# A decoder layer whose attention shares TensorE with projections: eight single-bank PSUM tiles in two sets that change places

## The chip, the cores and the metric

The kernel runs on one core of a Trainium2 chip. The core has a matrix engine (TensorE, called PE in the profile), a vector engine (DVE), an engine for activation functions (ACT), a general engine (POOL) and an engine that only issues transfers (SP). Matrix products are written into PSUM, a memory of eight banks of 2 KB for each of 128 partitions, so that one bank holds a tile of 128x512 in fp32. The metric is the time of one execution in device microseconds. Before the change it was 678.75 us (median of three, 678.59 to 678.98).

## The reference, cut to what matters

The kernel computes one pre-norm decoder layer for two sequences of 512 tokens and a width of 1024, in fp32:

```python
x = x + attention(layernorm(x))        # 32 query heads and 8 key heads of width 32, rope, causal
x = x + cross(layernorm(x), ctx)       # fake_quant(x) @ fake_quant(ctx), ctx is 1024x1024 per sequence
x = x + ffn(layernorm(x))              # x @ W_org.T + a mixture of 8 low-rank experts of rank 64

def attention(x):
    q, k, v = split(x @ w_qkv.T + b_qkv)                   # 1024, 256 and 256 columns
    scores = rope(q) @ rope(k).T / sqrt(32)                # each key head serves four query heads
    attn = softmax(where(causal, scores, -1e20))
    return (attn @ v) @ w_o.T + b_o
```

The change touches the attention and what runs beside it. The cross product and the feed-forward part fill the tail of the program; some of their units can also be used as filling work.

## The kernel before

**An order written by a planner.** The program does not leave the order to a scheduler. While it is built, a small model of the engines (class `Clocks`, line 99) keeps an estimated time for each engine, and the program text decides from it which instruction comes next. On the chip PE, DVE, ACT and POOL each execute their own list strictly in that order and wait on semaphores for one another. Work that is not TensorE's, such as rope, sums of weights and quantisation, lies in `lanes` of `Hop`s; `dispatch` (line 449) takes a hop when its engine is free and its operands are ready by the model, and `force` takes one at once. Work that is TensorE's and belongs to no slot lies in `queue` as generators; `step` (481) takes one matmul from the first generator that may start, `fill(us)` (527) adds to a `credit` and steps until it is spent, and `hold(us)` (535) steps until the model's PE clock has reached a time, so that PE doesn't stand still until then. When the queue has nothing, `hold` in the last slots draws from `last_resort`, a generator called `beside` with units of the second sequence's output product and other tail work.

**Chunks and slots.** The 32 heads of a sequence are handled as 8 chunks of 4 heads; with two sequences there are 16 chunks `g`. Four heads of width 32 use the 128 rows of TensorE together: four matmuls, each on 32 rows. Two chunks form a pair, and a pair takes five slots (`NS`), so that there are 40 slots (`n_slots`). The tables `QUERIES` and `KEYS` say which query tiles and key blocks a slot has; because of the causal mask a query tile `t` has `(t+1)*128` keys, and the slots are composed so that each covers 512 columns in all.

**One slot.** `scores(i)` (999) makes four score tiles `sc` (line 1016, queries by keys). DVE then adds the mask and takes each row's extreme, one instruction per head and part (`ms`, line 1029), and ACT exponentiates and sums (line 1039). When a chunk's slots are done, `split(g)` (1048) takes logarithms of the sums and splits them into three bf16 terms, in a chain over ACT, DVE and POOL; `turn_terms` (1069) transposes these by a DMA on ACT's queue to `mT`. Four slots later (`LAG`), `weights(i-4)` (1085) makes the transposed scores `st` (line 1098, keys by queries) and adds the terms by a matmul of `ones` with `mT` (line 1106), so that one exponential (line 1115, `pt`) gives normalised weights in the orientation that the next product needs. POOL clears the masked corner of the diagonal blocks (line 1118). `attend(g)` (1133) multiplies the weights with the values (`pv`, line 1141) and copies the result to `oT`.

**PSUM.** Three single banks (`ps_mm`) rotate among the filling work's products. One tile of four banks (`ps_sc`) is used by `sc` and `st` in turn; so `st` has to wait until DVE has read all of `sc`, and the next `sc` until ACT has read `st`. One bank (`ps_pv`) is for `pv`. Ahead of the loop and behind it, five further single banks stand in place of the last two pools. The function `mm` (370) hands out a bank for filling work, and `settle` forces its reader into the order if too many banks are unread.

**Filling work.** Queries, keys and values are projected by a Strassen–Winograd scheme, in units of four matmuls of 128x512 (`pj`, line 657, `quarter`), each added by DVE or copied by ACT. After them come the first sequence's output products (`wo`, in `g_tokens` line 1248, and `W_first` line 1726, which adds one chunk's contribution as soon as that chunk's values are there), and its quantised cross product (`cs`, `ct`). A unit may be half done when the slot's own matmuls interrupt it: in the loop, each slot runs `scores`, possibly `attend`, then `fill(rate * SLOT_S[j])`, then `weights`, then `fill(rate * SLOT_T[j])`.

Of the kernel before, what the change touches and what calls it, by code (L numbers as in the profile page):

```python
# [47 lines left out]
SLOT_S = (2.7, 3.2, 0.8, 2.7, 0.8)  # L48
SLOT_T = (1.8, 2.2, 2.2, 1.8, 2.2)
FILL_1 = 116.0  # L50
FILL_2 = 80.0
# [47 lines left out]
class Clocks:  # L99
# [6 lines left out]
    def __init__(self, nc):  # L106
        self.nc = nc
        self.seen = 0
        self.at = {"PE": 0.0, "DVE": 0.0, "Activation": 0.0, "Pool": 0.0, "DMA": 0.0}
        self.written = {}  # L110
        self.read = {}
        self.before = {}
        self.slots = {}
        self.used = {}
        self.tile_size = None

# [26 lines left out]
    def add(self, ins):  # L143
# [69 lines left out]
        for name, part in sources:  # L213
            self.read[name].add(part, done or end, engine)
        self.log(ins, engine, names, start)
# [6 lines left out]
def kernel(  # L222
# [58 lines left out]
    ps_mm = pool("ps_mm", 3, space=PSUM)  # L281
# [7 lines left out]
    beginning = ExitStack()  # L289
    ps_first = pool("ps_first", 5, beginning, space=PSUM)  # L290
# [66 lines left out]
    mm_pools = [ps_mm, ps_first, ps_first, ps_mm, ps_first, ps_first, ps_mm, ps_first]  # L357
    mm_count = [0]

    unread = []  # L360
    opened = [0]

    def settle(n):

        unread[:] = [key for key in unread if key not in done]
        while len(unread) > n:
            force(unread[0])
            unread[:] = [key for key in unread if key not in done]

    def mm(shape, name, dtype=F32):  # L370

        settle(2 if mm_pools[1] is ps_mm else 5)
        mm_count[0] += 1
        return mm_pools[mm_count[0] % len(mm_pools)].tile(shape, dtype, tag="mm", name=name)
# [24 lines left out]
    def transpose_f32(dst, t, src, name):  # L399

        for g in range(NK // 4):
# [5 lines left out]
            evacuate(dst[g][:, :, t * P : (t + 1) * P], ps)  # L407

# [68 lines left out]
    last_resort = [iter(())]  # L477
    weighted = [0]
    attended = [0]

# [19 lines left out]
    def may_start(key):  # L500
        if key == "post":
            return attended[0] >= NC - 1
# [24 lines left out]
    def fill(us):  # L527

        credit[0] += us
        while credit[0] > 0 and any_may():  # L530
            if not step():
                credit[0] = min(credit[0], 3.0)
                break

    def hold(us):

        while clocks.now("PE") + HOLD < us:
            if not (any_may() and step()) and next(last_resort[0], None) is None:
                break
# [99 lines left out]
    def add(col, dst, ps, other, key, bias=None, in_mm=True):  # L639
# [10 lines left out]
        if in_mm:  # L650
            unread.append(key)
# [14 lines left out]
    def g_kept(c, part=WHOLE, bank=None):  # L666
# [5 lines left out]
        if bank is None:  # L672
            unread.append(key)
# [3 lines left out]
        )  # L677

    def g_first(c, part=WHOLE, bank=None):
# [6 lines left out]
        add(c, dst[:, part], ps[:, part], place(c, 1, 0)[:, part], key, 0, bank is None)  # L686
        if last:
            complete(c, 0, 0, dst, key)

    def g_second(c):  # L690
# [7 lines left out]
        add(c, both, ps, both, ("U2", c))  # L698
        if c == COLUMNS[-1]:
# [5 lines left out]
        add(c, more, ps, both, ("U4", c))  # L705
        force(("S", 4))
# [4 lines left out]
        complete(c, 0, 1, dst, ("C12", c))  # L711

    def g_third(cols):

        for c in cols:
# [5 lines left out]
            add(c, more, ps, more, ("U7", c), 1)  # L721
            force(("T", c, 4))
# [3 lines left out]
            complete(c, 1, 0, both, ("C21", c))  # L726
        for c in cols:
# [9 lines left out]
    def g_values(b, halves_):  # L737
# [10 lines left out]
        for half, ps in zip(halves_, banks):  # L748
            evacuate(vs[b][:, :, half * P : (half + 1) * P], ps)
            if not b:  # L750
                q_live[0] -= 1

# [129 lines left out]
    banks = [mm([P, S], f"first_kv{i}") for i in range(4)]  # L882
# [16 lines left out]
    first_kv(slice(2 * P, S))  # L899

# [37 lines left out]
    settle(0)  # L938
    beginning.close()
    mm_pools[:] = [ps_mm] * 3  # L940
    ps_sc = pool("ps_sc", 1, attn, space=PSUM)
    ps_pv = pool("ps_pv", 1, attn, space=PSUM)
# [46 lines left out]
    last_sc = [None]  # L989

    def sc_free():

        clocks.catch_up()
        return clocks.read[last_sc[0].name].last() if last_sc[0] is not None else 0.0

# [3 lines left out]
    def scores(i):  # L999


        pair, j = divmod(i, NS)
        sc = ps_sc.tile([P, 4, S], F32, tag="sc", name=f"sc{i}")
        parts = []
        at_col = 0
# [1130 lines left out]
```

## Time and profile before

| | |
|---|---|
| time, median of three | 678.75 us (678.59 to 678.98) |
| the profiled execution: span from first to last instruction | 675.4 us |
| what lies around that span, against the median | 3.35 us |
| granted TensorE clock, mean | 0.996 |
| first scores of the loop start | 45.8 us |
| last scores of the loop start | 376.6 us |
| last values (`pv`) end | 409.7 us |
| busy PE / DVE / ACT / POOL | 647.2 / 504.2 / 299.3 / 93.5 us |

The profile has one execution of the program, taken by the hardware profiler. The profiled execution's own time is its span of 675.4 us; the small rest up to the median lies ahead of the first and behind the last instruction. An operation's line gives its source line, the engine, and output and inputs by the program's names, with shapes as partitions x elements; behind the bar stand its total busy time, the mean duration of one in ns, and the idle time of its engine just before it with what ended that. In the timeline the first column is the start, the second the time until the group's end, `x8` the number of instructions that stand side by side, and a bracket the idle time before them. An fp32 matmul appears as two records because it takes two passes.

The whole has three parts. The lead-in to 45.8 us normalises the input and makes the first projections. The attention loop runs to 409.7 us. The tail does what is left: the second sequence's output product, most of the cross product and the feed-forward part.

### The profile page before, as it was taken

What the parts mean: (1) busy time and instruction counts of PE and PEld (TensorE: products, weight loads), DVE (VectorE), ACT (ScalarE), POOL (GpSimd) and SP (SyncE); (2) the same over time, 40 slices, a digit from 0 to 9 for tenths busy, and PEclk for the clock granted to TensorE, in tenths of its full rate; (3) what the DMA queues carried; (4) which work ended last, traced back from release to release, by engine and by line L of the source; (5) the groups of instructions that cost most, each with busy time, mean ns of one, the idle gap of its engine ahead of it and who ended that gap; (6) DMA issues with size and microseconds to landing.
All of it is one profiled execution on the core that took longest, in us unless ns stands there. A gap on an engine that the chain in (4) does not pass through costs nothing.

```text
span 675.4 us, 8962 instructions
## 1 busy us (share of the span) xinstructions
PE 647.2 (96%) x3197; PEld 294.5 (44%) x3204; DVE 504.2 (75%) x1205; ACT 299.3 (44%) x695; POOL 93.5 (14%) x213
## 2 busy tenths in 40 slices
PE   5999689999999999999989999999999999999997
PEld 5754233343433434334434444444445454444443
DVE  5799689976678989777678657898969944743775
ACT  2245465666776486877767731354221100110100
POOL 2100023312222122122222321000001000000000
PEclk9999899999999999999999999999999999999999
DMA  9930000010103352102100208295100003000104
GB/s 288 324 74 0 8 9 1 9 40 9 39 2 102 101 134 40 65 14 50 24 10 1 24 9 287 93 333 97 20 28 0 1 31 124 1 0 0 63 0 186
DMA packets 42476, 44.63 MB, mean 66 GB/s; under 512 B 19264, under 2 KB 32576, under 8 KB 42432
## 3 DMA queue, kind: packets, MB, share of 16 engines
q1 hardware_dynamic: 24992, 38.82, 17.3%
q10 hardware_dynamic: 17440, 5.25, 4.8%
q8 instruction: 25, 0.41, 0.3%
q14 instruction: 19, 0.16, 0.1%
HBM read 35.66 MB, written 4.19 MB: 59 GB/s over the span
## 4 chain that ended last, share of the span: by engine, by line
PE 70%; ACT 15%; DVE 12%; issue 1%; DMA 0%; POOL 0%; ACTq 0%; DVEq 0%; POOLq 0%
PE wb L1599 14%; ACT ms L1039 8%; PE pj L657 8%; PE wo L1599 7%; PE up L1682 7%; PE h L1646 7%; ACT pt L1115 7%; DVE ms L1029 5%; PE sc L1016 5%; PE st L1098 3%; PE ct L1248 3%; PE wo L1248 3%; PE first_kv L657 2%; PE pj_v L657 2%; PE pv L1141 2%; PE pj_k L657 1%
## 5 line engine op out<-in xcount | busy, mean ns | idle before, releaser
L1039 ACT ACTIVATE ms<-ms,stats 128x512 f32<-128x512 f32 (+3 forms) x256 | 140.2, 549 | 84.0 <-DVE stats L1029 81.5
L1029 DVE CUSTOM_DVE_ANT_0 ms<-sc,mask 128x512 f32<-128x512 f32 (+3 forms) x256 | 108.3, 485 | 34.8 <-PE sc L1016 31.8
L1115 ACT ACTIVATE pt<-st 128x2048 f32<-128x2048 f32 x40 | 74.8, 1870 | 38.3 <-PE st L1106 38.1
L657 PE MATMUL pj<-xT,wq 128*128 128x512 f32 x192 | 90.9, 606 | 0.0
L1118 POOL TENSOR_SCALAR_AFFINE_SELECT pt<-pt 128x512 f32<-128x512 f32 x64 | 47.4, 757 | 245.2 <-ACT pt L1115 245.2
L1098 PE MATMUL st<-qT,kT 32*128 32x128 f32 (+3 forms) x512 | 49.5, 461 | 4.9 <-DVE stats L1029 4.8
L657 PEld LDWEIGHTS pj<-xT,wq 128*128 128x128 f32 x192 | 33.8, 189 | 40.3 <-issue 39.7
L1016 PE MATMUL sc<-kT,qT 32*128 32x128 f32 (+3 forms) x512 | 45.8, 460 | 4.1 <-ACT pt L1115 1.4
L1039 ACT ACTIVATION_READ_ACCUMULATOR ms<-ms,stats 128x1 f32 x256 | 47.8, 187 | 0.0
L1248 PE MATMUL wo<-wo,oT 128*128 128x512 f32 x96 | 46.6, 613 | 0.0
L1016 PEld LDWEIGHTS sc<-kT,qT 32*128 32x128 f32 x512 | 22.4, 184 | 39.6 <-ACT pt L1115 26.5
L1141 PE MATMUL pv<-pt,v 128*32 128x128 f32 (+3 forms) x512 | 37.8, 436 | 0.0
L1098 PEld LDWEIGHTS st<-qT,kT 32*128 32x128 f32 x512 | 21.1, 185 | 32.6 <-DVE stats L1029 18.8
L1248 PE MATMUL ct<-q,q1T 128*128 128x512 bf16 x123 | 28.0, 379 | 1.3 <-DVE oT L382 0.8
L1599 PE MATMUL wb<-tb,S 128*128 128x512 f32 x64 | 28.3, 595 | 0.0
L1599 PE MATMUL wb<-worg,S 128*128 128x512 f32 x64 | 28.0, 592 | 0.0
L1599 PE MATMUL wb<-worg,x3T 128*128 128x512 f32 x64 | 27.8, 592 | 0.0
L1141 PEld LDWEIGHTS pv<-pt,v 128*32 128x32 f32 x512 | 14.9, 109 | 29.3 <-issue 20.6
L1248 PEld LDWEIGHTS wo<-wo,oT 128*128 128x128 f32 x96 | 16.7, 189 | 21.0 <-issue 20.3
L657 PE MATMUL pj_k<-xT,wk 128*128 128x512 f32 x32 | 17.2, 667 | 5.6 <-DVE qT L648 5.6
L648 DVE TENSOR_TENSOR qT<-pj,qT 128x512 f32<-128x512 f32 x28 | 18.8, 683 | 4.2 <-PE pj L657 4.2
L1189 ACT ACTIVATE raw<-raw,qp_sb,inv_s 128x1024 f32<-128x1024 f32 x8 | 9.8, 1237 | 25.3 <-DMA raw<-in_ctx_dram 24.0
(235 smaller groups left out, 1017.6 us busy)
## 6 DMA issues: line engine op xcount, KB each, us to landing
wq<-in_wqT_dram SPq DMA_DIRECT2D x8, 512.0 KB, 8.7
ctx_raw<-in_ctx_dram SPq DMA_DIRECT2D x8, 512.0 KB, 3.3
wo<-in_woT_dram SPq DMA_DIRECT2D x8, 512.0 KB, 3.3
raw<-in_ctx_dram SPq DMA_DIRECT2D x8, 512.0 KB, 5.7
worg<-in_worgT_dram SPq DMA_DIRECT2D x8, 512.0 KB, 7.1
out_dram<-x SPq DMA_DIRECT2D x16, 256.0 KB, 2.1
x<-in_x_dram SPq DMA_DIRECT2D x7, 512.0 KB, 6.0
x_raw<-in_x_dram SPq DMA_DIRECT2D x4, 512.0 KB, 7.5
```

The costliest lines, as they stand in the source:

```text
L657: nc.tensor.matmul(ps[:, part], weight[:, k, :], xs_[:, k, part], start=(k == 0), stop=(k == n - 1),)
L1016: nc.tensor.matmul(sc[:, s, part], qTs[b, c][row(s), t * P : (t + 1) * P], kTs[b][row(s), c // 4, :klen], start=True, stop=True,)
L1029: nc.vector.tensor_tensor_reduce(out=ms, in0=sc[:, s, part], in1=mask[:, S - klen :], scale=-scale, scalar=BIG, op0=ALU.add, op1=ALU.min, ...
L1039: nc.scalar.activation(ms, ms, AF.Exp, bias=least, scale=-1.0, accum_out=stats[g][:, t, s, 1:2],)
L1098: nc.tensor.matmul(sc[:, s, part], kTs[b][row(s), c // 4, kb * P : (kb + 1) * P], qTs[b, c][row(s), kb * P :], start=True, stop=False,)
L1115: nc.scalar.activation(pt, sc[:, :, :n], AF.Exp, scale=scale)
L1118: nc.gpsimd.affine_select(out=diagonal, in_=diagonal, compare_op=ALU.is_ge, fill=0.0, base=0, pattern=[[0, 4], [1, P]], channel_multiplier=-1,
L1141: nc.tensor.matmul(pv[row(s), kb * P :], vs[b][:, kb, h * HD : (h + 1) * HD], pt[:, s, part], start=(kb == 0), stop=(kb == NT - 1),)
L1248: nc.tensor.matmul(ps, l[:, t * P : (t + 1) * P], r[:, cols], start=(k == 0), stop=(k == len(terms_) - 1))
L1599: nc.tensor.matmul(ps[i], l[:, k, i * P : (i + 1) * P], r(k), start=(k == 0), stop=(k == n - 1))
L1646: nc.tensor.matmul(ps[i], r(k)[:, i * P : (i + 1) * P], l[:, k, :], start=(k == 0), stop=(k == n - 1))
L1682: nc.tensor.matmul(ps[t], l[:, k, t * P : (t + 1) * P], r(k), start=(k == 0), stop=(k == n - 1))
```

## The change

The three PSUM pools become one pool of eight single-bank tiles, `sets[0][0..3]` and `sets[1][0..3]`. Each slot becomes one `visit(i)`. In a visit, `scores(i)` goes into the set called `new`, one head per bank, and `weights(i-4)`, the transposed scores, directly behind it into the set called `old`, which is where the filling units ran since the last visit. Then, head by head, come DVE's minimum and ACT's exponential of the new scores, and ACT's exponential of the transposed scores, now four of 128x512 in place of one of 128x2048. If a chunk's values are due, `pv` goes into the first bank of `new` after DVE's minimum of head 0 has been written into the order. From then to the next visit, filling units may use only the banks of `new`, and only whole units run there: generators yield `CLOSED` at their end, and `close()` steps until no bank is half written. The next visit swaps the sets.

The bookkeeping is changed with it. `take_bank` marks a bank as open, `read_by` names the lane's hop that will read it, and `empty` forces those readers before a set is used. `fill` is given a cycle time less the visit's own share, and rounds to whole units; `hold` adds a unit only if the model's PE clock is more than `HOLD` and half a unit early. The other changes: `post`, the work behind the first sequence's attention, may start only when all eight chunks are attended (before: seven); `W_first` is gone, and every output product of the first sequence is made in two halves of four matmuls with a DVE add each; `last_resort` is gone from `hold`; the loop ends with visits 40 to 43, which hold only transposed scores and values.

Its core as a diff:

```diff
-SLOT_S = (2.7, 3.2, 0.8, 2.7, 0.8)
-SLOT_T = (1.8, 2.2, 2.2, 1.8, 2.2)
-FILL_1 = 116.0
-FILL_2 = 80.0
+VISIT, VALUES = 2.35, 2.35
+CYCLE_1, CYCLE_2 = 7.5, 7.1
+UNIT = 3.44
...
-    ps_mm = pool("ps_mm", 3, space=PSUM)
+    psum = pool("psum", 1, space=PSUM)
...
+    sets = [
+        [psum.tile([P, 512], F32, tag=f"bank{n}{i}", name=f"bank{n}{i}") for i in range(4)]
+        for n in range(2)
+    ]
...
+    def is_free(place):
+
+        n, i = place
+        key = reader.get(place)
+        if key is None or key in done:
+            return True
+        return key is OPEN and clocks.bank_read[sets[n][i].name] >= taken[place]
+
+    def empty(places):
+
+        for place in places:
+            if not is_free(place):
+                assert reader[place] is not OPEN, place
+                force(reader[place])
...
     def may_start(key):
         if key == "post":
-            return attended[0] >= NC - 1
+            return attended[0] >= NC
...
     def fill(us):
 
         credit[0] += us
-        while credit[0] > 0 and any_may():
+        while any_may() and (is_open() or credit[0] > UNIT / 2):
             if not step():
-                credit[0] = min(credit[0], 3.0)
+                credit[0] = min(credit[0], UNIT)
                 break
 
+    def close():
+
+        while is_open():
+            step()
+
     def hold(us):
 
-        while clocks.now("PE") + HOLD < us:
-            if not (any_may() and step()) and next(last_resort[0], None) is None:
-                break
+        while clocks.now("PE") + HOLD + UNIT / 2 < us and any_may() and step():
+            close()
...
-        pt = ptp.tile([P, 4, n], F32, tag=f"pt{j % 3}", name=f"pt{i}")
-        nc.scalar.activation(pt, sc[:, :, :n], AF.Exp, scale=scale)
+
+    def terms_of(i, sc):
+
+        parts = turned(i)
+        n = parts[-1][2].stop
+        pt = ptp.tile([P, 4, n], F32, tag=f"pt{i % NS % 3}", name=f"pt{i}")
+        for s in range(4):
+            nc.scalar.activation(pt[:, s, :], sc[s][:, :n], AF.Exp, scale=scale)
+            yield
...
+        many = len(terms_) if how == "ctx" else len(terms_) // 2
+        for first in range(0, len(terms_), many):
+            part = terms_[first : first + many]
+            ps = mm([P, 512], f"{name}{b}_{t}_{h}")
...
-        hold(when([pts[g, n][0] for n in range(NT)]))
-        attend(g)
-
-    for i in range(n_slots + LAG - 1):
+
+    filler = [0]
+
+    def visit(i):
+
         pair, j = divmod(i, NS)
-        if i == n_slots:
-            last_resort[0] = beside
...
+        old, new = filler[0], 1 - filler[0]
+        g = 2 * pair + j // 2 - 3 if j in (2, 4) else -1
...
+        close()
+        when_free = [last_read((new, s)) for s in range(4)]
         if i >= LAG:
-            of = {2 * ((i - LAG) // NS) + n for n, _ in KEYS[(i - LAG) % NS]}
-            for g in sorted(of):
-                force(("mT", g))
-            hold(max([sc_free()] + [when([mT[g]]) for g in of]))
-            weights(i - LAG)
+            of = {n for n, _, _ in turned(i - LAG)}
+            for n in sorted(of):
+                force(("mT", n))
+            when_free += [when([mT[n]]) for n in of]
+        hold(max(when_free))
+        empty([(old, s) for s in range(4)])
+        of = {}
+        sc, st = sets[new], sets[old]
+        if i < n_slots:
+            scores(i, sc)
+        if i >= LAG:
+            weights(i - LAG, st)
+        exponentials = terms_of(i - LAG, st) if i >= LAG else iter([None] * 4)
+        for s in range(4):
+            if s == 1 and g >= 0:
+                pv = take_bank((new, 0))
+                attend(g, pv)
+            if i < n_slots:
+                least_of(i, sc, s, of)
+                total_of(i, s, of)
+            next(exponentials)
+        for _ in exponentials:
+            pass
+        if g >= 0:
+            attended_to(g, pv)
+        filler[0] = new
+        allowed[:] = [(new, s) for s in range(4)]
         dispatch()
-        fill(rate * SLOT_T[j])
-        hold(sc_free())
+        fill((CYCLE_1 if i <= n_slots // 2 + LAG else CYCLE_2) - VISIT - VALUES * (g >= 0))
...
-    weights(n_slots - 1)
+
+    for i in range(n_slots + LAG):
+        visit(i)
+    close()
+    empty(every)
...
     run_some(4)
-    attend(last - 1)
+    pv = mm([P, S], "pv")
+    attend(last - 1, pv)
+    attended_to(last - 1, pv)
     run_some(5)
```

The order of the instructions in the two programs differs accordingly: in the changed one, 36 times `st` follows `sc` with nothing between, and all units stand whole. The number of passes through TensorE is the same.

## The prediction

> **What bounds the kernel now.** First the page's busy row, its clock row and its chain of work that ended last:
>
> ```profile
> PE 647.2 (96%) x3197; PEld 294.5 (44%) x3204; DVE 504.2 (75%) x1205; ACT 299.3 (44%) x695; POOL 93.5 (14%) x213
> ...
> PEclk9999899999999999999999999999999999999999
> ...
> PE 70%; ACT 15%; DVE 12%; issue 1%; DMA 0%; POOL 0%; ACTq 0%; DVEq 0%; POOLq 0%
> ```
>
> TensorE is the bound at nearly full clock, but 27% of the chain passes through ACT and DVE. The windows' table cuts the span at the first scores (45.8) and at the end of the last values (409.7):
>
> ```profile
> 0.00:45.80 45.80, 38.52 (x196) 28.45 (x196) 34.41 (x80) 12.76 (x25) 7.42 (x21) 1.00 0.86 253
> 45.80:409.70 363.90, 347.81 (x2305) 146.84 (x2308) 277.65 (x819) 240.17 (x608) 80.83 (x183) 1.00 0.14 33
> 409.70:675.40 265.70, 260.89 (x701) 119.19 (x700) 192.16 (x307) 46.38 (x62) 5.30 (x9) 1.00 0.24 79
> ```
>
> The middle stage holds all that is changed. Its busy PE is not all streaming; TensorE's timeline shows what a block of matmuls takes:
>
> ```profile
> 118.43 0.93 PE L1098 MATMUL st<-qT,kT 32*128 32x384 f32 x8 [1.02 <-DVE stats L1029]
> 119.18 0.34 PE L1106 MATMUL st<-mT,onesb 3*128 3x384 bf16 x4
> 119.35 0.40 PE L1098 MATMUL st<-qT,kT 32*128 32x128 f32 x8
> 119.57 0.24 PE L1106 MATMUL st<-mT,onesb 3*128 3x128 bf16 x4
> ...
> 121.84 1.15 PE L1016 MATMUL sc<-kT,qT 32*128 32x384 f32 x16
> 122.92 1.12 PE L657 MATMUL pj<-xT,wq 128*128 128x512 f32 x2
> 123.97 2.36 PE L1141 MATMUL pv<-pt,v 128*32 128x512 f32 x32
> 126.26 1.13 PE L657 MATMUL pj<-xT,wq 128*128 128x512 f32 x2
> 127.32 1.14 PE L1098 MATMUL st<-qT,kT 32*128 32x512 f32 x8
> ```
>
> Weight loads inside a long run of projections come every 0.43 us (0.19 busy, 0.24 idle), so one fp32 pass is 0.43 and a unit of four matmuls (eight passes) 3.43. Two passes between scores and values need 0.86 but take 1.05 (122.92 to 123.97): a change of the kind of matmul costs about 0.21. The key blocks of one `st` are neighbours, and show no such cost. Without it a slot's `sc` needs 0.85, `st` with its ones 1.07, one `pv` 2.13.
>
> The stage needs 184.8 of filling work (projections, output weights, quantised matmuls and transposes, their passes counted in the order of instructions) + 40×0.85 + 40×1.07 + 16×2.13 = 295.7. I count 176 changes of kind, 176×0.21 = 37. So 363.9−295.7−37 = 31 us are waits. By engine the waits are:
>
> ```profile
> ACT pt L1115 <- PE st L1106: 38.1, 20, 7.1
> ...
> DVE ms L1029 <- PE sc L1016: 31.8, 21, 4.3
> ...
> PEld sc L1016 <- ACT pt L1115: 26.5, 29, 1.2
> ```
>
> ACT and DVE wait for PE more than PE for them; `sc` waits for the exponential that frees the one four-bank tile, at most 1.2 us, because half-finished units stand between. One long wait is bad for another reason:
>
> ```profile
> 78.56 4.40 PE L657 MATMUL pj_k<-xT,wk 128*128 128x512 f32 x6 [3.68 <-DVE qT L648]
> ```
>
> Six records take 4.40 there (0.73 each) where 0.43 is usual: the granted clock is half until about 83.1, which is the 8 in the clock row. That costs about 1.7 us on top of the wait. [...]
>
> **The change, part by part.**
>
> *Fewer changes of kind.* In after's order `st` follows `sc` directly (36 times, kinds alike, taken at 0 as between key blocks; at 0.21 it would be +7.6), and units are whole. 95 costing changes remain: 95×0.21 = 20, a gain of 17 us.
>
> *Work moved.* 9.4 us of filling work (two of the quantised blocks and transposes) falls behind the loop: the stage needs 286.3, the tail 256.9+9.4 = 266.3. Neutral in itself. The tail's own 8.8 of waits and changes are kept. The tail receives part of the eight more DVE adds (each half of a W tile now has its own, 0.60 each, +4.8 on DVE in all); DVE is busy 192 of 266 us there and PE 261, so PE covers them; uncovered, +4.8. The lead-in loses banks (four, then eight, against eight): taken at 0, bounds −1 and +3 (its idle PE is 45.8−38.5 = 7.3, mostly on x and its norms). SP has the same transfers; the 16 transposes on ACT's queue (2.4 us to landing) stand behind up to eight exponentials, priced below.
>
> *The split exponential.*
>
> ```profile
> L1115 ACT ACTIVATE pt<-st 128x2048 f32<-128x2048 f32 x40 | 74.8, 1870 | 38.3 <-PE st L1106 38.1
> L1118 POOL TENSOR_SCALAR_AFFINE_SELECT pt<-pt 128x512 f32<-128x512 f32 x64 | 47.4, 757 | 245.2 <-ACT pt L1115 245.2
> ```
>
> One of 128x2048 holds ACT 1.77 start to next start; four of 128x512 have no row. Lower bound: a quarter each, 0.45. Upper: ACT's copy of 128x512 out of PSUM, 0.58. Taken 0.49 (that copy's start-to-start is 0.48): 1.96 a visit, +0.19 a visit, at most +0.55. It counts only where ACT ends a visit. [...]
>
> *The new wait.* Before, a unit could be half done while `st` waited; after, between visits only whole units run, into the banks that `sc` has just left, and the next `sc` needs the banks of the previous `st`, freed by its exponentials, which now alternate with the score exponentials on ACT. Score exponentials run every 0.71 a head at 512 columns (0.61, and 0.09 for the accumulator read) and 0.98 where a head has two parts (235.25 to 236.23 in ACT's timeline: 0.39 and 0.60). ACT's block per visit is 4×(0.71+0.49) = 4.8 or 4×(0.98+0.49) = 5.9. The first exponential starts 1.8 to 2.06 after its `sc`, so the next `sc` cannot finish its last head before about 6.5 or 7.7. PE's own work is 0.85+1.07+0.22 = 2.15 a visit, 4.5 with `pv`, plus 3.43 a unit and 0.2: with two units 9.2 (covered), with `pv` and one unit 8.2 (covered), with one unit 5.8 (short by 0.7 to 1.9), with none 2.1 or 4.5 (short by 2 to 5). After's order gives the units: 16 visits have two, 15 have one or a little more (3.4 to 4.7 us), nine have half a unit or less. Carried from visit to visit with these numbers:
> - exponentials: visits 12, 13, 17, 23, 24 and 35 to 38 follow thin ones and wait 1.7, 2.7, 1.9, 1.9, 4.4, 1.3, 2.2, 1.2, 0.6: 18 us. Visits 22 and 23 are thin because the first half's output weights now wait for the eighth chunk's values, where before they followed each chunk's.
> - `st` waits for DVE's add of the last unit (0.6 to 0.7, queued behind rope and ctx rows of 0.6 to 0.8): mostly 0.3 to 0.9, once 2.6: 10 us. What is queued on DVE behind that add are the minima of the next visit.
> - visits 0 to 3: a unit waits for the minima to read a bank, behind DVE's weight and x sums: 9 us.
> - `mT` landing: 2.
>
> In the loop 39; last scores at 45.8+333 (328 to 339 as I vary the exponential, the DVE load and the 0.21), against 376.6 before.
>
> *The end.* Before, 33 us from the last `sc` to the end of the last `pv`, 16.6 of filling work in it. After has only 3.4 (one output unit): the exponentials of visit 39 end at 7.7, the terms 3.1 later (384.23 to 387.29 before), the transpose lands at 13.3; then `st` 1.2, exponentials 2.0, two selects 1.5 (0.757 each), `pv` 2.4, `st` 1.3, exponentials 2.1, selects 1.5, `pv` 2.3: 27.5. PE needs 15.2 of that: 12 us of waits. Two stops (visit 24, the wait for `mT`) exceed 3.5 us and should halve the clock as at 78.56: 2×1.7 = 3.4.
>
> **The sum**, with W for the stage's waits: 45.8 + 286.3 + 20 + W + 266.3 + 8.8 = 627.2 + W. Before's own 31 would give 658.2; W = 39+12+3.4 = 54 gives 681.6, against 675.4. The profiled execution lies 3.35 under the median of 678.75, so about **685 us**. Break-even is W = 48.
>
> **Rivals.**
> 1. *Waits stay under 46: faster, 662 to 677.* For: the waits' table, where ACT idles 38 us for PE and PE little for ACT; and the 39 is a hand recurrence in which a late head delays everything behind it. If the 9 us of visits 0 to 3 fall by 6 and the 18 halve, W = 39: a span of 666, a time of 669.5. Against: visits with no unit have nothing else to run, whatever the order. It decides at W = 48.
> 2. *ACT's chain sets the loop: 692 to 703.* Exponentials at 0.58 add 0.36 in the dozen or so visits that ACT ends (+4.3), the DVE adds lose their cover (+4.8), the clock drops at four more stops (+6.8): 685+16 = 701. Against: DVE and ACT have long idle times in before.
> 3. *The change does little: 677.4 to 680.1.* Fewer changes of kind and the emptied end cancel: W = 47 to 49.
>
> **How the numbers follow.** 0.2% (1.4 us) is about what a measurement of this kernel can tell from no change. Forecast (680.1 to 692) 0.48; rival 1 0.31; rival 2 0.15; rival 3 0.06. The likeliest is 685, its own range 680 to 692. For 8 in 10 the range runs from 668 (rival 1 without its lowest fifth) to 699 (rival 2 with its three extras not all together). Faster 0.31, same 0.06, slower 0.63.
>
> **What would show it.** Right: PE idle in the stage beyond 20 us, most of it before `sc`, released by ACT's split exponential at visits 12, 13, 17, 23, 24 and 35 to 38, and a gap of some 4 us at visit 24; four exponentials of 0.55 to 0.6 duration a visit; `sc` and `st` back to back without the 0.2; last `sc` near 379, last `pv` near 406; tail near 275; an 8 or lower in the clock row near 250 and 390. Wrong: last `sc` before 370 (waits over-counted), `sc` to `st` costing 0.2 (+7.6), a tail over 280 (DVE adds uncovered), or the clock staying full through the end.

## The result, and the profile after

The changed kernel takes 711.65 us (median of four runs, 710.9 to 714.23) against 678.67 us before: 1.0493 times as long, with an interval of 1.0463 to 1.0522. The direction of the forecast (slower, 685 us) was right. The size was not: the loss is 33 us where 6 were forecast, and the time lies outside the range of 668 to 699.

The page of the changed kernel, its busy row, its clock row and its chain (the same rows as those shown of before):

```profile
PE 677.2 (95%) x3198; PEld 318.9 (45%) x3204; DVE 507.7 (71%) x1210; ACT 307.5 (43%) x818; POOL 89.2 (13%) x213
...
PEclk9999999997999996999999879999999999999999
...
PE 78%; DVE 10%; ACT 8%; issue 2%; DMA 1%; POOL 0%; ACTq 0%; SPq 0%; DVEq 0%; POOLq 0%
```

ACT's share of the chain has halved, from 15% to 8%, and TensorE's has grown from 70% to 78%. Read alone, that looks like a gain, but the time is longer. The clock row says one reason: a 7, a 6, an 8 and a 7 stand where before had one 8. In those slices the granted clock was 0.71, 0.69, 0.83 and 0.75 on the mean, and 0.50 for part of the time, so some of its larger share is work at half speed.

The windows' table of the changed kernel, cut at the first scores and at the end of the last values:

```profile
0.00:45.78 45.78, 37.97 (x197) 28.02 (x197) 34.50 (x80) 12.08 (x24) 7.44 (x21) 1.00 0.84 253
45.78:435.80 390.02, 368.82 (x2258) 166.02 (x2260) 275.98 (x815) 245.81 (x726) 75.88 (x182) 0.95 0.11 31
435.80:710.20 274.40, 270.42 (x749) 124.82 (x748) 197.24 (x316) 49.57 (x68) 5.87 (x10) 1.00 0.23 77
```

The lead-in is unchanged. The tail is 8.7 us longer, which is the work that moved there (9.4 forecast). The attention stage is 26.1 us longer, although it holds 9.2 us less work. The granted clock of the stage, third column from the end, is 0.95.

The place where the first 7 of the clock row comes from, in TensorE's timeline of the changed kernel (visits 12 to 14; start, length, operation, idle before):

```profile
151.13 1.32 PE L1071 MATMUL bank<-kT,qT 32*128 32x256 f32 x6
153.22 0.91 PE L1071 MATMUL bank<-kT,qT 32*128 32x256 f32 x9 [0.77 <-ACT pt L1172]
...
155.35 2.36 PE L1198 MATMUL bank<-pt,v 128*32 128x512 f32 x32
157.64 2.07 PE L1071 MATMUL bank<-kT,qT 32*128 32x512 f32 x4
160.06 1.12 PE L1071 MATMUL bank<-kT,qT 32*128 32x512 f32 x2 [0.34 <-ACT pt L1172]
161.52 1.22 PE L1071 MATMUL bank<-kT,qT 32*128 32x512 f32 x1 [0.34 <-ACT pt L1172]
...
165.66 6.52 PE L707 MATMUL bank<-oT,t 128*128 128x512 f32 x8
172.01 3.60 PE L707 MATMUL bank<-xT,wq 128*128 128x512 f32 x8
```

Visit 12 has no unit of filling work between its values (155.35) and the next scores (157.64). Those scores then come one head at a time: each waits until ACT has freed its bank. Four heads that need 0.85 us together take from 157.64 to beyond 162. Nothing here is an idle stretch of 3 us; TensorE runs one head on 32 of its 128 rows, waits 0.34, runs the next. Yet the granted clock falls at 161.1 and returns at 171.4, and the unit at 165.66 takes 6.52 us where the next takes 3.60. The windows' table, cut at these times (third column from the end: the granted clock):

```profile
157.71:161.12 3.41, 3.07 (x7) 0.81 (x6) 0.69 (x1) 3.41 (x13) 0.00 (x0) 1.00 0.00 0
161.12:171.36 10.24, 9.90 (x34) 5.11 (x34) 5.70 (x15) 6.77 (x16) 3.56 (x10) 0.50 0.06 13
171.36:175.00 3.64, 3.64 (x9) 1.52 (x8) 1.29 (x2) 0.00 (x0) 0.00 (x0) 1.00 0.41 144
```

In the first of these windows ACT is busy for all 3.41 us, and TensorE waits for it. But ACT's own timeline shows that ACT waits in its turn just before and behind: for the scores (through DVE's minimum) and for the transposed scores, which wait for ACT:

```profile
154.55 0.51 ACT L1098 ACTIVATE ms<-ms,stats 128x256 f32<-128x256 f32 x1 [1.38 <-DVE stats L1083]
...
163.04 0.72 ACT L1098 ACTIVATE ms<-ms,stats 128x512 f32<-128x512 f32 x1 [1.22 <-DVE stats L1083]
...
165.72 0.60 ACT L1172 ACTIVATE pt<-bank 128x512 f32<-128x512 f32 x1 [1.87 <-PE bank L1158]
```

It is a ring: last exponential of the old visit, last head of the new scores, transposed scores behind it on TensorE, first exponential of these, and so on. With a unit or two in between, the ring has slack. Without one, every link is on the path.

The waits of the changed kernel that matter here (engine, line, releaser: us in total, times, longest):

```profile
ACT ms L1098 <- DVE stats L1083: 119.0, 40, 6.5
...
DVE ratio L1118 <- ACT ratio L1116: 47.1, 15, 3.5
...
PEld bank L1071 <- ACT pt L1172: 18.5, 23, 1.2
...
DVE ms L1083 <- PE bank L1071: 17.0, 16, 5.4
...
ACT pt L1172 <- PE bank L1198: 15.6, 15, 3.0
...
PEld bank L1150 <- DVE qT L699: 5.9, 8, 1.2
...
PE bank L1158 <- DMA mT<-terms: 4.5, 1, 4.5
```

The wait of the scores' loads for `pt` was 26.5 us in 29 waits before; it has not grown in sum. What has changed is where it stands, in a few visits in a row with nothing else to run. DVE's wait for `ratio` is 47.1 us in 15 waits; it comes back below. In the waits' table of before it was:

```profile
DVE ratio L1059 <- ACT ratio L1057: 14.2, 7, 3.5
```

A sum over the stage, each visit's length less the streaming time of its matmuls at full clock (0.43 us for an fp32 pass of 512 columns, as between the weight loads of before), gives:

| us | before | after |
|---|---|---|
| stage | 363.9 | 390.0 |
| streaming at full clock | 305.1 | 295.9 |
| changes of the kind of matmul | 176 x 0.21 = 37 | 95 x 0.21 + 36 x 0.11 = 24 |
| streaming done at half clock (its extra time) | 1.7 | 14.8 |
| the rest: waits | 20 | 55 |

The price of 0.21 for a change of kind is the forecast's. Visits 5, 11, 16 and 25 of the changed kernel, which hardly wait, leave 0.18 for one; at that price the waits would be 25 before and 58 after.

For the changed kernel the excess over streaming is 94.1 in all; 45.0 of it stands in five places: visits 13 (9.2), 23 (4.3), 24 (8.6), 37 (7.5), and from visit 39 to the last values (15.5). Four of the five follow a visit with half a unit or less; ahead of visit 37 two visits have half a unit each and one has 3.2 us. The other 35 visits have 1.4 each. Those with hardly a wait have 0.5 to 0.6, for the changes of kind; many others wait 0.9 more in `st`. One of these, TensorE's timeline of the changed kernel:

```profile
209.70 1.36 PE L1071 MATMUL bank<-kT,qT 32*128 32x512 f32 x8
210.66 1.42 PE L1150 MATMUL bank<-qT,kT 32*128 32x384 f32 x5
211.50 0.33 PE L1158 MATMUL bank<-mT,onesb 3*128 3x384 bf16 x1
...
212.78 7.13 PE L707 MATMUL bank<-xT,wq 128*128 128x512 f32 x16
```

`sc` starts 0.96 before `st`, that is 0.11 over its 0.85: here the step from `sc` to `st`, both on 32 rows, costs 0.11, less than the 0.21 of a change of kind, but not nothing. `st` then takes from 210.66 to 212.78, 2.12 where 1.2 is usual, because one of its banks still holds the last unit's result. DVE's timeline of the changed kernel says why that is added so late:

```profile
210.28 0.34 DVE L1118 TENSOR_TENSOR ratio<-ratio,stats 128x16 f32<-128x16 f32 x1 [3.38 <-ACT ratio L1116]
...
210.74 0.68 DVE L699 TENSOR_TENSOR qT<-bank,qT 128x512 f32<-128x512 f32 x1
```

The unit is done at 209.7, but on DVE its add stands behind a step of the chunk's `split`, which waits 3.38 us for ACT, and ACT takes that step only after the visit's eight exponentials. So the order of DVE passes ACT's delay on to TensorE, once for each chunk.

### The profile page after: what moved, and what is told of

It reads as the page before. It is cut to its first block, busy times and chain, and to the rows that moved or that the text cites. A ratio compares the mean times of both kernels' runs of the same rounds, so it can differ in the third digit from the quotient of the medians.

```text
span 710.2 us, 9224 instructions
## 1 busy us (share of the span) xinstructions
PE 677.2 (95%) x3198; PEld 318.9 (45%) x3204; DVE 507.7 (71%) x1210; ACT 307.5 (43%) x818; POOL 89.2 (13%) x213
## 4 chain that ended last, share of the span: by engine, by line
PE 78%; DVE 10%; ACT 8%; issue 2%; DMA 1%; POOL 0%; ACTq 0%; SPq 0%; DVEq 0%; POOLq 0%
PE bank L1665 20%; PE bank L707 15%; PE bank L1314 10%; PE bank L1748 7%; PE bank L1712 7%; PE bank L1150 6%; PE bank L1071 5%; PE bank L1198 5%; ACT ms L1098 4%; ACT pt L1172 3%; DVE ms L1083 2%; PE bank L450 2%; PE bank L1158 2%; DVE sh_q L629 1%; DVE qT L699 1%
## 5 line engine op out<-in xcount | busy, mean ns | idle before, releaser
L1083 DVE CUSTOM_DVE_ANT_0 ms<-bank,mask 128x512 f32<-128x512 f32 (+3 forms) x256 | 108.2, 486 | 17.2 <-PE bank L1071 17.0
L1172 ACT ACTIVATE pt<-bank 128x512 f32<-128x512 f32 x160 | 92.7, 588 | 23.6 <-PE bank L1198 15.6
L707 PE MATMUL bank<-xT,wq 128*128 128x512 f32 x192 | 87.6, 599 | 3.2 <-DVE stats L1083 3.2
L1150 PE MATMUL bank<-qT,kT 32*128 32x384 f32 (+3 forms) x512 | 73.1, 474 | 6.1 <-DVE oT L427 1.7
L1071 PE MATMUL bank<-kT,qT 32*128 32x128 f32 (+3 forms) x512 | 68.5, 474 | 5.8 <-ACT pt L1172 5.8
L1314 PE MATMUL bank<-wo,oT 128*128 128x512 f32 x128 | 57.9, 603 | 0.0
L707 PEld LDWEIGHTS bank<-xT,wq 128*128 128x128 f32 x192 | 34.9, 190 | 42.7 <-issue 36.5
L1071 PEld LDWEIGHTS bank<-kT,qT 32*128 32x128 f32 x512 | 31.4, 188 | 48.9 <-ACT pt L1172 18.5
L1150 PEld LDWEIGHTS bank<-qT,kT 32*128 32x128 f32 x512 | 35.5, 195 | 26.0 <-DVE qT L699 5.9
L1198 PE MATMUL bank<-pt,v 128*32 128x128 f32 (+3 forms) x512 | 43.8, 489 | 0.0
L1158 PE MATMUL bank<-mT,onesb 3*128 3x512 bf16 (+3 forms) x256 | 34.6, 315 | 4.5 <-DMA mT<-terms 4.5
L1118 DVE TENSOR_TENSOR ratio<-ratio,stats 128x16 f32<-128x16 f32 x16 | 4.8, 301 | 47.1 <-ACT ratio L1116 47.1
L1314 PEld LDWEIGHTS bank<-wo,oT 128*128 128x128 f32 x128 | 23.7, 192 | 28.2 <-issue 26.7
```

The source lines that it names most:

```text
L707: nc.tensor.matmul(ps[:, part], weight[:, k, :], xs_[:, k, part], start=(k == 0), stop=(k == n - 1),)
L1071: nc.tensor.matmul(sc[s][:, part], qTs[b, c][row(s), t * P : (t + 1) * P], kTs[b][row(s), c // 4, : (t + 1) * P], start=True, stop=True,)
L1083: nc.vector.tensor_tensor_reduce(out=of[s][:, part], in0=sc[s][:, part], in1=mask[:, S - (t + 1) * P :], scale=-scale, scalar=BIG, op0=ALU ...
L1150: nc.tensor.matmul(sc[s][:, part], kTs[b][row(s), c // 4, kb * P : (kb + 1) * P], qTs[b, c][row(s), kb * P :], start=True, stop=False,)
L1158: nc.tensor.matmul(sc[s][:, part], onesb[32 * s : 32 * s + 3, :], mT[g][32 * s : 32 * s + 3, kb * P :], start=False, stop=True,)
L1172: nc.scalar.activation(pt[:, s, :], sc[s][:, :n], AF.Exp, scale=scale)
```

## The experiments

Theory A: the loss comes from visits that have too little filling work, where scores and exponentials wait for each other in the ring, and from the clock that halves after them. Theory B: the split exponential loads ACT, whatever the order. Further rivals stand with each run. Ratios are to the kernel before, measured on the same chip in the same batch.

**The exponentials of the transposed scores early.**

```diff
             if i < n_slots:
                 least_of(i, sc, s, of)
                 total_of(i, s, of)
-            next(exponentials)
-        for _ in exponentials:
-            pass
+            if s == 0:
+                for _ in exponentials:
+                    pass
```

> The changed kernel with one edit: in a visit, ACT takes the four exponentials of the transposed scores right after the first score exponential instead of alternating with all four. Theory A (the loss comes from visits with little filling work, where the next scores wait head by head for the last of the interleaved exponentials, and from the clock that halves after such visits): the waits before the scores shrink from the 18 us released by the exponential to under 6, fewer than four half-clock stretches remain, and the time is 690 to 702 us against 711.65. Theory B (ACT's amount of work per visit sets the loop, whatever its order, because four exponentials of 128x512 replaced one of 128x2048): within 3 us of 711.65. The planner also sees the earlier exponentials and moves some units, which is part of the run.

Measured: 703.32 us, 1.0368 (1.0325 to 1.0411); the half-clock time of the stage falls from 41.0 to 20.5 us, and the wait of the scores' loads for `pt` falls from 18.5 to 3.2 us. B's figure is refuted, and A's upper end of 702 is missed by 1.3 us: there are still four half-clock stretches, though short ones. The planner moved units as well, from visit 4 on, and a new wait of 6.9 us for rope stands before visit 25, so the 8 us are not the order's alone.

**Added work that nobody reads.**

```diff
         fill((CYCLE_1 if i <= n_slots // 2 + LAG else CYCLE_2) - VISIT - VALUES * (g >= 0))
+        for n in range({12: 1, 22: 1, 23: 1, 36: 1, 39: 1, 40: 1}.get(i, 0)):
+            ps = mm([P, 512], f"dummy{i}_{n}")
+            for k in range(4):
+                nc.tensor.matmul(ps, ident, kTs[0 if i < 20 else 1][:, 0, :], start=(k == 0), stop=(k == 3))
+            reader[of_name[ps.name]] = None
```

> The changed kernel with six further units of TensorE work that nobody reads (four matmuls of 128x512 each, identity times keys; the outputs stay as they are), one at the end of visits 12, 22, 23, 36, 39 and 40, so 6 x 3.43 = 20.6 us of added TensorE work. Theory A (those visits stand waiting, and the four half-clock stretches follow from TensorE being thinly used, not from a long idle stretch): the added work lies in the waits and keeps the clock at full, so the time rises by much less than the work or falls: 700 to 713 us, with a mean clock above 0.985. Theory C (the time went into the order itself and the clock costs little): 720 to 732 us.

Measured: 702.62 us, 1.0358 (1.0319 to 1.0398). With 20.6 us more work on TensorE, the kernel is 9 us faster than without. The planner sees the added units; DVE's and ACT's orders are those of the changed kernel up to 258 us, and differ behind it. The profile's own line for it (span and mean granted clock):

```profile
core 0: 701.4 us, clock 0.992
```

And the same place as above, visits 12 and 13 of this kernel (L1975 is the added unit):

```profile
157.96 3.70 PE L1975 MATMUL bank<-kT,ident 128*128 128x512 f32 x8
161.59 1.36 PE L1071 MATMUL bank<-kT,qT 32*128 32x512 f32 x8
...
163.98 3.70 PE L707 MATMUL bank<-oT,t 128*128 128x512 f32 x8
```

The added unit takes the place of the waits between heads; the scores run together in 0.97 us; and the unit behind them takes 3.70 where it took 6.52. From the values of visit 12 to the scores of visit 14 the changed kernel needs 20.2 us, this one 15.4, with a unit more and all else in the same order. Theory A holds there; of the 9 us as a whole, a part may be the new order behind 258 us.

**The same added work on a quarter of the rows.** The order of the instructions on every engine is that of the run before; only the rows differ. The edit is against that run; `clocks.whole` makes the planner price the units as if they used all rows.

```diff
+            clocks.whole = True
+            rows_ = row(of_name[ps.name][1])
             for k in range(4):
-                nc.tensor.matmul(ps, ident, kTs[0 if i < 20 else 1][:, 0, :], start=(k == 0), stop=(k == 3))
+                nc.tensor.matmul(
+                    ps, ident[rows_, :], kTs[0 if i < 20 else 1][rows_, 0, :], start=(k == 0), stop=(k == 3)
+                )
...
+            clocks.whole = False
```

> The run with six added units once more, in the same order of all instructions on every engine, but the added matmuls use 32 of TensorE's 128 rows (one head's row tile) instead of all; each still takes its two passes of 512 columns, so TensorE is occupied as long as there. If the clock follows how much of the array is in use (theory A in its sharper form): the half-clock stretches that the added units removed come back, the mean clock falls under 0.985, and the time is 706 to 716 us against 702.6. If the clock follows only whether a matmul is running: 701 to 705 us and the same clock, 0.992.

Measured: 710.25 us, 1.048 (1.0453 to 1.0508); the intervals of the two runs do not meet. The profile's line of span and clock, and the same place in TensorE's timeline (L1979 is the added unit):

```profile
core 0: 706.0 us, clock 0.985
```

```profile
157.12 2.41 PE L1979 MATMUL bank<-kT,ident 32*128 32x512 f32 x5
...
165.12 6.36 PE L708 MATMUL bank<-oT,t 128*128 128x512 f32 x8
171.32 3.60 PE L708 MATMUL bank<-xT,wq 128*128 128x512 f32 x8
```

Half-clock stretches are back at 160 and 266, behind visits 12 and 23, where the full-row units had removed them, and the unit at 165.12 again takes 6.36. The windows' table on both sides of the first fall:

```profile
156.86:160.27 3.41, 3.41 (x23) 1.72 (x17) 0.69 (x1) 3.41 (x14) 0.00 (x0) 1.00 0.00 0
160.27:170.51 10.24, 10.24 (x39) 5.71 (x36) 5.80 (x15) 7.09 (x18) 3.41 (x10) 0.50 0.07 13
```

TensorE is busy for all 3.41 us of the first of these windows, and its granted clock falls from 1.00 to 0.50 at the end. In the run with all rows TensorE has no wait at the same place either (3.70 for the added unit from 157.96, then the scores), and the unit at 163.98 takes 3.70. So what made the difference in this pair is not whether a matmul was running but that the added ones used 32 rows instead of 128. The streaming done at half clock rises from 4.7 to 9.2 us; the rest of the 7.6 us is not taken apart. The last of these units run beside the next scores on other rows (in its timeline, one from 159.37 to 159.96 and one of the scores from 159.48 to 160.07), which by itself would make this run faster, not slower.

**The split exponential alone, in the kernel before.**

```diff
-        nc.scalar.activation(pt, sc[:, :, :n], AF.Exp, scale=scale)
+        for s in range(4):
+            nc.scalar.activation(pt[:, s, :], sc[:, s, :n], AF.Exp, scale=scale)
```

> The kernel before with one part of the change alone: the exponential of 128x2048 is made as four of 128x512 at the same place. If ACT's load is on the path (theory B), 40 x 0.2 to 0.3 us: 686 to 691 us against 678.7. If it is only felt in visits with little filling work (theory A), within 2 us of 678.7.

Measured: 708.62 us, 1.0454 (1.0407 to 1.05). Neither theory has that. Its trace shows a line that has nothing to do with exponentials, at the start of the tail:

```profile
441.42 4.84 PE L1600 MATMUL wo<-to,S 128*128 128x512 f32 x6 [9.03 <-DVE x L1255]
```

The planner had priced four exponentials higher than one, and ordered everything anew. So the same split was made once more, with the planner told that the four are one (its model takes the four together and charges them as before; the edit's core):

```diff
...
+        if engine == "Activation" and outs[0].tensor.name.startswith("pt"):
+            self.held.append((names, sources))
+            if len(self.held) < 4:
+                return
+            names = [x for pair in self.held for x in pair[0]]
+            sources = [x for pair in self.held for x in pair[1]]
+            self.held = []
+            heads = 4
...
+            many = max([n] + [_free(a) for a in ins_]) * heads
...
```

> The kernel before with the exponential of 128x2048 made as four of 128x512, and the planner told that they are one, so that the order of all other instructions is that of the kernel before, on every engine. The earlier run of the same split, where the planner chose a new order, took 708.6 us. If the four exponentials themselves cost that (ACT's load on the path): 700 us or more. If the new order did (a stall of 9 us at the start of the tail and two more half-clock stretches are in its trace): 676 to 683 us, that is at most 40 x 0.19 us on top of the kernel before.

Measured: 682.96 us, 1.0066 (1.0053 to 1.0079). DVE, POOL and the rest of ACT keep the order of the kernel before. The split costs 4.4 us there, 0.11 a slot. The other 26 us of the first attempt came from the new order. In the changed kernel the price can be read directly: in the group below four of them take 4 x 0.588 busy, and in ACT's timeline one starts 0.48 before the next instruction, close to the 0.49 of the forecast:

```profile
L1172 ACT ACTIVATE pt<-bank 128x512 f32<-128x512 f32 x160 | 92.7, 588 | 23.6 <-PE bank L1198 15.6
...
207.85 0.58 ACT L1172 ACTIVATE pt<-bank 128x512 f32<-128x512 f32 x1
208.33 0.50 ACT L1098 ACTIVATE ms<-ms,stats 128x256 f32<-128x256 f32 x1
```

**The emptied end alone, in the kernel before.**

```diff
-        if i == n_slots:
-            last_resort[0] = beside
```

> The kernel before with one part of the change alone: the last slots get no filling work from the second output product (the last resort is gone, as in the change). Theory A (the emptied end is one part of the loss): the waits of the last 33 us that this work filled come to light and the clock falls there, so 684 to 692 us. Rival (that work only moved out of the tail, where it costs the same, and the waits at the end are short): within 2 us of 678.7.

Measured: 680.75 us, 1.0035 (1.0012 to 1.0058), so 2.4 us by the ratio: far from theory A's 684, and just outside the rival's 2 us. TensorE's order is that of the kernel before up to 391 us. The last resort as such matters little; of the 16.6 us that fill the end in before, 6.8 are its output product (L1599), and the larger part comes from the ordinary queue.

**Spreading the units.** Three runs put the same real work into other visits. The first takes the exponentials early, has at least one unit a visit and `CYCLE_1` 6.9; the second asks for 3.1 us instead of one unit; the third adds unread units where none is left. The edits are against the changed kernel, cut to what is new in each.

```diff
-        while any_may() and (is_open() or credit[0] > UNIT / 2):
+        least = credit[0] - UNIT / 2
+        while any_may() and (is_open() or credit[0] > min(UNIT / 2, least)):
...
```

> The changed kernel with the exponentials of the transposed scores taken early (as in the first of these runs), at least one unit of filling work in every visit that can have one, and the first cycle constant at 6.9 instead of 7.5. Only visits 39 to 41 are left without a unit; the work is the same. Theory A: no half-clock stretch before visit 39, waits before the scores under 10 us: 682 to 694 us. If the early exponentials' own order or DVE sets the loop: 700 us or more.

Measured: 690.99 us, 1.0171 (1.0144 to 1.0197). As expected in time, not in the clock: there are stretches at 193, 326 and 347, 3.4 us each, behind visits with one unit or half a unit, and one of 10.2 us at 398.

```diff
+        start = credit[0]
-        while any_may() and (is_open() or credit[0] > UNIT / 2):
+        while any_may() and (is_open() or credit[0] > UNIT / 2 or start - credit[0] < least_us[0]):
...
+        least_us[0] = 0.9 * UNIT if g >= 0 else 0.9 * UNIT
```

> As the run with at least one unit in every visit (691 us), but the least is 3.1 us of filling work instead of one unit, because units of the bf16 product are only 1.7 us long: visits 31 to 34, which had 1.7, 1.7, 6.8 and 3.4 us and lost two half-clock stretches' worth, get 3.4, 3.4, 6.8 and 3.4. Theory A: the half-clock stretches at 326 and 347 us and their waits of 4 to 5 us in visits 32 and 34 go: 682 to 687 us. If thin visits don't matter there: 690 to 692 us.

Measured: 686.9 us, 1.0127 (1.0091 to 1.0163). The stretches at 326 and 347 are gone; the one at 193 stays, and that of the end has 13.7 us.

```diff
+        for n in range({23: 1, 39: 1, 40: 1, 41: 1}.get(i, 0)):
+            ps = mm([P, 512], f"dummy{i}_{n}")
...
```

> The same with four added units that nobody reads (13.7 us of TensorE work on all rows) at the end of visits 23, 39, 40 and 41, where no real unit is left. Theory A: visit 23 costs up to 3 us more, the others lie in the waits of the end, whose half-clock stretch of 10 us goes (2.7 us of streaming lost there): between 3 us faster and 2 us slower than the run without them. If the end is limited by TensorE's own work: 10 us slower or more.

Measured: 686.07 us, 1.0108 (1.0077 to 1.0138): 13.7 us of added work change the time by less than a microsecond, with DVE, ACT and POOL in the same order as without, and the mean clock is 0.998. TensorE's timeline of its end (L1979 are added units):

```profile
389.31 3.70 PE L1979 MATMUL bank<-kT,ident 128*128 128x512 f32 x8
...
394.25 3.70 PE L1979 MATMUL bank<-kT,ident 128*128 128x512 f32 x8
...
400.21 0.29 PE L1161 MATMUL bank<-mT,onesb 3*128 3x256 bf16 x4 [1.08 <-DMA mT<-terms]
...
401.37 3.60 PE L1979 MATMUL bank<-kT,ident 128*128 128x512 f32 x8
```

In the run without the added units the same wait for `mT` is 7.61 us:

```profile
398.24 0.40 PE L1161 MATMUL bank<-mT,onesb 3*128 3x256 bf16 x4 [7.61 <-DMA mT<-terms]
```

In the changed kernel it is 4.51 us, and the matmuls behind it run at a granted clock of 0.50 (`pv` takes 4.30 where it took 2.36):

```profile
420.91 0.40 PE L1158 MATMUL bank<-mT,onesb 3*128 3x256 bf16 x4 [4.51 <-DMA mT<-terms]
...
423.38 4.30 PE L1198 MATMUL bank<-pt,v 128*32 128x512 f32 x32
```

**Real work in the place of the added.** If 13.7 us are free there, real units held back from earlier visits should gain. Three runs hold some visits at one unit (25, 30, 35; then also 28 and 33; then all of 24 to 38):

```diff
+        kept = credit[0]
+        if i in (25, 30, 35):
+            credit[0] = -1e3
         fill((CYCLE_1 if i <= n_slots // 2 + LAG else CYCLE_2) - VISIT - VALUES * (g >= 0))
+        if i in (25, 30, 35):
+            credit[0] = kept
...
-        hold(max(when_free))
+        if i - 1 not in (25, 30, 35):
+            hold(max(when_free))
```

> As the run of 686.9 us with at least 3.1 us of filling work in each visit, but visits 25, 30 and 35 are held at one unit where they had two. The units saved stand in visits 38 to 41, where added units that nobody read cost nothing. Theory A (the work is only in the wrong visits): 2 x 3.43 us of the end's waits are used and its half-clock stretch of 14 us goes: 676 to 682 us. Rival (visits without values and with one unit are limited by ACT's chain, so that the loop gets no shorter): 685 us or more.

> The same with visits 25, 28, 30, 33 and 35 held at one unit. 13.7 us leave the loop's first 40 visits, some 12 us stand in visits 40 to 42. Theory A: 672 to 680 us, under or about the kernel before. Rival (ACT's chain limits neighbouring one-unit visits): each of the five held visits gains nothing, 680 us or more.

> The same with all visits 24 to 38 held at one unit, so every visit from 24 to 42 has exactly one, and 3.4 us more of the work falls into the tail than in the run with five. Theory A with ACT's chain at 6 to 7 us a visit: visits without values fall below it and wait 1 to 2 us each: 674 to 684 us, no faster than the run with five held visits.

Measured: 685.93 (1.0107, 1.0077 to 1.0136), 684.12 (1.0085, 1.006 to 1.011) and 684.87 us (1.0103, 1.0077 to 1.013). They gain 1 to 3 us on 686.9, where theory A had 676 to 682, 672 to 680 and 674 to 684. The rival's times hold in the first two; the third is 0.9 us over its range and, as expected, no faster than the second. That ACT's chain is the limit, as the rival says, is not shown by them. In the run with five held visits, visit 27 has a wait that two units had covered:

```profile
278.57 1.14 PE L1153 MATMUL bank<-qT,kT 32*128 32x512 f32 x8 [1.47 <-DVE x L1324]
```

`st` waits for DVE's add of the last unit, which stands behind rope and rows of the cross product in DVE's order. Visits 25 to 33 of that run have 0.6 to 2.4 us of excess each, but visits 35 to 37, with one unit each as well, only 0.5 to 1.1. In the profiled executions of the first and third run new half-clock stretches stand at 330 and 368, and at 305 and 380. None of the versions beats the kernel before; the best, at 684.12, is 0.85% slower.

## Why the prediction was wrong, point by point

The forecast put the last scores near 379 and the last values near 406; they are at 404.3 and 435.8. The tail (275 forecast, 274.4) and the lead-in were right, so the error of the span (710.2 against 681.6) is the stage's: 390.0 us against 360.7, 29.3 more. In time the error is 26.7, because the 3.35 us added between span and median were too much: the runs that list both have 1.7 to 2.0 us outside the span (711.96 against 710.2 here), so the profiled execution of before was itself somewhat faster than the median. By the terms of the sum:

- **"The stage needs 286.3" was too low by 9.6.** The streaming counted from the trace is 295.9, and 305.1 before where the forecast had 295.7. I had counted the filling work short, in both programs by about the same amount. In the account of before the error hid in the waits (31, really 22 with the clock); in the sum of after, whose waits were carried from visit to visit, it did not cancel. The forecast gave two units to 16 visits, about one to 15 and half or less to nine; the trace has 19, 13 and eight. Three units more are 10 us.
- **"Two stops should halve the clock: 2x1.7 = 3.4" was too low by 11.4.** This is the step that failed as a mechanism. The forecast read one row of before, a wait of 3.68 us with 3.41 us at a granted clock of 0.50 behind it, and expected as much of each stop of over 3.5 us. No run shows that limit, and the 1.7 a stop is an estimate from that one row. The trace of the changed kernel showed in its place four stretches at 0.50, of 10.2, 13.7, 6.8 and 10.2 us, and none begins behind such a stop: before the end, no wait of TensorE in the stage is longer than 1.43 us, and the fourth fall, at 417.1, comes 0.7 us into the wait for `mT` of 4.51. They stand at visits 13, 24 and 37 and at the wait for `mT`; two of the four (24 and the end) had been named. Streaming of 14.8 us fell into them. Even in the row of before the clock fell only at 79.71, 1.15 us after TensorE had started again (at 78.56).
- **`sc` to `st` "taken at 0" costs 0.11**, 4 us in all; the end of 0.21 that was kept for the range would have been 7.6.
- **The waits, "39 in the loop and 12 at the end", are 55 against 51.** The ring of exponentials, the wait of `st` for DVE's add, the first four visits and the end were named with the right places: the visits 12, 13, 17, 23, 24 and 35 to 38 do wait for `pt` (the last only in its weight loads, 0.6). That the total is close is in part luck: with 0.6 a visit taken off for the changes of kind, an estimate, these nine visits wait some 25 us where 18 were forecast, and the first four some 4 where 9 were.
- **The split exponential at 0.49** was right (0.48), but that it counts only where ACT ends a visit is not shown: in the kernel before it cost 4.4 us.
- **Rival 2** (ACT's chain with more drops of the clock, 692 to 703) was nearest. It still priced a drop at 1.7 us and expected it at stops.

The four terms make 9.6 + 11.4 + 4 + 4 = 29, against 29.3. The range failed for the same reasons: rival 2, which set its upper end, allowed four more drops at 1.7 us each, and nothing for a miscount.

## What to carry to other kernels

When work is arranged so that one engine's units fill another's waits, look at the emptiest intervals, not at the mean: four of forty visits and the end held nearly half of the excess. A clock row with single digits under 9 is a cost to be priced before it is explained (here 14.8 us), and added work on all rows, placed in waits, was free or better than free here: 13.7 us of it changed one run by less than 1 us, and 20.6 us made another 9 us faster. Where an order is planned from a cost model, a small edit changes the whole order; keep the order fixed to price the edit (4.4 us), or the new order is what is measured (31 us).

## What the runs showed of the hardware

In the changed kernel the granted clock fell without a long idle stretch ahead of it. It was 0.50 from 161.12 to 171.36, from 263.52 to 277.17, from 389.81 to 396.64 and from 417.12 to 427.36 us, 41.0 us in all. Around the first three falls (160 to 162, 262.5 to 264.5 and 388.5 to 390.5) no wait of TensorE is longer than 0.34, 0.69 and 0.95 us; the fourth comes 0.7 us into a wait of 4.51. In the loop of the kernel before it was 0.50 once, from 79.71 to 83.12.

The pair of runs with added units has the same order of instructions. With these units on all 128 rows the mean clock was 0.992 and the time 702.62 us; on 32 rows they were 0.985 and 710.25 us, and from 160.27 to 170.51 the clock was 0.50. So in this pair the clock depended on the rows in use. What in general lowers it, and what brings it back, is not shown by these runs.
